# Turning the residual back behind a second batch norm: two more groups of transposes in the waits, products nobody reads between them, and a shorter chain of small operations

## The chip, the core and the metric

The kernel runs on one core of a Trainium2 chip. The metric is the device time of one execution in microseconds (us), the median of several runs. All numbers are float32.

## The reference, cut to what matters

Four graph layers run one after the other on x of shape (128 batches, 64 nodes, 256 features), each as x = x + layer(relu(layernorm(x))). The change sits where the third layer ends and the fourth begins:

```python
# layer 2 (the third)
h = relu(layernorm(x))
agg = A_hat @ h                                   # per batch, 64 x 64
h = relu(batchnorm(agg @ W1.T + b1, g1, be1))     # 512 features
out = batchnorm(h @ W2.T + b2, g2, be2)           # 256 features
x = x + out
# layer 3 (the fourth)
h = relu(layernorm(x))
h = relu(weighting @ (h @ W1)); h = relu(weighting @ (h @ W2)); y = weighting @ (h @ W3)
x = x + y
```

A batch norm takes the mean and variance of a feature over all 8192 tokens. So no token of layer 2 is finished before the last token has gone through its second product: this is a barrier, and layer 3 cannot start before it.

## The kernel before, in words

The 8192 tokens are cut into 16 groups of 512 tokens. x stays in the on-chip memory, tokens on the partitions (tiles `xs[g]`, 4 blocks of 128 tokens by 256 features). Layer 2 works with the features on the partitions: its output tile for group g, `outs[g // 2]`, holds 2 chunks of 128 features by 512 tokens, so that mean and variance are sums along a row.

For each group, the loop of layer 2 applies the first batch norm with its relu on ScalarE (L1039), multiplies on TensorE (L1049, two chunks m), takes the statistics of each product on VectorE (`bn_stats`, L1058) and moves it out of PSUM with its bias on ScalarE (L1059). In the last group the products are sorted so that chunk 0 is complete first. `bn_finish` (L968 on) then makes a scale `sc` and a shift `sh` for each chunk: `bn_aggr`, add eps (L977), power -0.5 on GpSimd (L978), add the bias to the mean (L980), times gamma (L981), mean times scale (L982), beta minus that (L983). The same function finishes the first batch norm (4 chunks) earlier.

Behind the barrier, for each group:

- `normalize(g)` applies scale and shift in place, chunk 0 on ScalarE (L1072), chunk 1 on VectorE (L1075). These two are kept in program order.
- `to_residual(g)` transposes the result back to tokens on the partitions (8 transposes of 128x128 on TensorE, L1085, into two PSUM banks) and adds each bank to `xs[g]` on VectorE (L1089).
- `start(g)` does the layer norm of `xs[g]` (statistics on VectorE at L92 to L98, a power on GpSimd at L96, the scaling with relu on ScalarE at L111, or for one block of group 0 on VectorE at L105 and L109), then the first mix with the weighting (64x64 products, L143) and its two copies out of PSUM (L155, one on VectorE, one on ScalarE). Group 0 is done in two halves of 256 tokens.
- `first_weights`, `second_mix`, `second_weights`, `third_weights`, `last_mix` and `finish` are the rest of layer 3. Each weight product is done as seven smaller products: four first (1, 5, 6, 7), of which 1 and 5 are copied to `p1` and `p5` on ScalarE (L171, L172), then 2, 3 and 4 into the same banks, with sums on VectorE (L174, L175, L183, L187), on GpSimd (L178) and relus on ScalarE (L214, L217).

`bring(n, ahead)` (L1250) puts `to_residual` of n groups and `normalize` of further groups between these stages. Before the first weights of group 0, groups 1 to 3 are normalised, and their 24 transposes stand behind the first four of the seven products; groups 4 and 5 follow behind the second mix, 6 and 7 behind the second weights.

Two resources matter for the order. PSUM has 8 banks, handed out in turn by `bank()`. The pool `ar_right` has 8 tiles, and all of them hold `outs`; the tile `m1` that `first_weights` of group 0 writes `p1` and `p5` into is the tile of groups 0 and 1 of `outs`, free when both have been transposed.

Instructions are issued by each engine in the order that the scheduler wrote down; `issue_after` keeps a stretch behind an instruction.

Of the kernel before, what the change touches and what calls it, by code (L numbers as in the profile page):

```python
# [9 lines left out]
AF = mybir.ActivationFunctionType  # L10
ALU = mybir.AluOpType
# [3 lines left out]
P = 128  # L15
D = 256
# [22 lines left out]
def adj_preln_kernel(ctx: ExitStack, tc: tile.TileContext, x_in, adj, vec, bg0, bg1,  # L39
# [9 lines left out]
    def bank(shape=(P, 512)):  # L49
        return psp.tile(list(shape), F32, tag="ps", name="ps")  # L50
# [50 lines left out]
    def ln_apply(src, dst, rstd, nmr, n=GT, on_vector=()):  # L101

        for t in range(n):
            if t in on_vector:
                nc.vector.tensor_scalar(  # L105
                    dst[:, t, :], src[:, t, :], rstd[:, t : t + 1], nmr[:, t : t + 1],
                    ALU.mult, ALU.add,
                )
                nc.vector.tensor_scalar(dst[:, t, :], dst[:, t, :], 0.0, None, ALU.max)  # L109
                continue  # L110
            nc.scalar.activation(  # L111
                dst[:, t, :], src[:, t, :], AF.Relu,
                bias=nmr[:, t : t + 1], scale=rstd[:, t : t + 1],
            )

    def ln_relu(src, dst, between=None):

# [10 lines left out]
                )  # L128
        return pss

    def mix(src, a2, chunks, dst, copies, swap=False):

        for c0 in range(0, chunks, 2):
            pss = [bank((P, 2, GT, NODES)) for _ in range(2)]
            for t in range(GT):
                for c in range(2):
                    for half in range(2):
                        for b in range(2):  # L140
                            rows = slice(b * 64, b * 64 + 64)
                            col = (c0 + c) * P + half * 64
                            nc.tensor.matmul(  # L143
                                pss[b][half * 64 : half * 64 + 64, c, t, :],
                                lhsT=src[rows, t, col : col + 64],
                                rhs=a2[rows, :],
                                start=True, stop=True,
                            )
            for b in range(2):
                if swap:  # L150
                    to = dst[:, c0 : c0 + 2, :].rearrange("p c (k b m) -> p b c k m", b=2, m=P)
                    last = copies[b](to[:, b], pss[b].rearrange("p c (k q) n -> p c k (q n)", q=2))
                else:
                    to = dst[:, c0 : c0 + 2, :].rearrange("p c (t b n) -> p b c t n", b=2, n=NODES)
                    last = copies[b](to[:, b], pss[b])  # L155
        return last.ins
# [45 lines left out]
    def sums(eng, a11, a12, a21, a22, s1, s2, s3, s4):  # L202

        eng.tensor_tensor(out=s1, in0=a21, in1=a22, op=ALU.add)
        eng.tensor_tensor(out=s2, in0=s1, in1=a11, op=ALU.subtract)
        eng.tensor_tensor(out=s3, in0=a11, in1=a21, op=ALU.subtract)
        eng.tensor_tensor(out=s4, in0=a12, in1=s2, op=ALU.subtract)

    def ends_in(out, func):

# [757 lines left out]
    def bn_finish(st, n, v_0, v_g, v_b, tag):  # L968


        scs, shs = [], []
        for m in range(n):
            mv = bp.tile([P, 2], F32, tag=f"{tag}mv{m}", name=f"{tag}mv{m}")
            sc = bp.tile([P, 1], F32, tag=f"{tag}sc{m}", name=f"{tag}sc{m}")
            sh = bp.tile([P, 1], F32, tag=f"{tag}sh{m}", name=f"{tag}sh{m}")
            nc.vector.bn_aggr(mv, st[:, m].rearrange("p g s -> p (g s)"))
            nc.vector.tensor_scalar(sc, mv[:, 1:2], BN_EPS, None, ALU.add)  # L977
            nc.gpsimd.tensor_tensor(out=sc, in0=sc, in1=mhalf[:, 0:1], op=ALU.pow)  # L978
            mean = mv[:, 0:1]
            nc.vector.tensor_tensor(mean, mean, vecs[:, v_0 + m : v_0 + m + 1], ALU.add)  # L980
            nc.vector.tensor_tensor(sc, sc, vecs[:, v_g + m : v_g + m + 1], ALU.mult)  # L981
            nc.vector.tensor_tensor(sh, mean, sc, ALU.mult)  # L982
            nc.vector.tensor_tensor(sh, vecs[:, v_b + m : v_b + m + 1], sh, ALU.subtract)  # L983
            scs.append(sc)
            shs.append(sh)
        return scs, shs
# [49 lines left out]
    for g in range(NG):  # L1036
        a = h1s[g]
        for m in range(4):
            nc.scalar.activation(  # L1039
                a[:, m, :], a[:, m, :], AF.Relu,  # L1040
                bias=sh1[m], scale=sc1[m],
            )
        pss = [bank() for _ in range(2)]
        order = [(c, m) for c in range(4) for m in range(2)]
        if g == NG - 1:

            order.sort(key=lambda cm: cm[1])
        for c, m in order:
            nc.tensor.matmul(  # L1049
                pss[m], lhsT=w2[c // 2][:, c % 2, m * P : (m + 1) * P], rhs=a[:, c, :],  # L1050
                start=(c == 0), stop=(c == 3),
            )

        if g % 2 == 0:
            outs.append(arena(ar_right))
        o = outs[-1][:, 2 * (g % 2) : 2 * (g % 2) + 2, :]
        for m in range(2):
            nc.vector.bn_stats(st2[:, m, g, :], pss[m])  # L1058
            nc.scalar.activation(  # L1059
                o[:, m, :], pss[m], AF.Identity, bias=vecs[:, V_B2 + m : V_B2 + m + 1]  # L1060
            )
        if g == NG - 4:
            w_three = layer3_weights()
    sc2, sh2 = bn_finish(st2, 2, V_B2, V_G2, V_BE2, "n2")

    b1, t1s, a2, s2s, b3, t3s = w_three

    def normalize(g, tok=slice(0, GN)):

        o = outs[g // 2][:, 2 * (g % 2) : 2 * (g % 2) + 2, tok]  # L1070
        tc.keep_in_program_order(
            nc.scalar.activation(o[:, 0, :], o[:, 0, :], AF.Identity, bias=sh2[0], scale=sc2[0])  # L1072
        )
        tc.keep_in_program_order(
            nc.vector.tensor_scalar(o[:, 1, :], o[:, 1, :], sc2[1], sh2[1], ALU.mult, ALU.add)  # L1075
        )

    def to_residual(g, ks=range(2)):
        o = outs[g // 2][:, 2 * (g % 2) : 2 * (g % 2) + 2, :]
        for k in ks:  # L1080
            ps = bank((P, 2, D))
            for t in range(2):
                tok = (2 * k + t) * P
                for c in range(2):
                    nc.tensor.transpose(  # L1085
                        ps[:, t, c * P : (c + 1) * P], o[:, c, tok : tok + P], ident
                    )
            xk = xs[g][:, 2 * k : 2 * k + 2, :]
            nc.vector.tensor_tensor(xk, xk, ps, ALU.add)  # L1089


    def start(g, behind):


        a = arena(ar_left)
        h = a[:, 0:2, :].rearrange("p a (b d) -> p (a b) d", d=D)
        if g == 0:

            for k in range(2):
                two = slice(2 * k, 2 * k + 2)  # L1100
                with tc.issue_after(scaled) if k else nullcontext():
                    to_residual(0, [k])
                    rstd, nmr, scaled = ln_scale(xs[0][:, two], None, 2, True)
                    ln_apply(xs[0][:, two], h[:, two], rstd, nmr, 2, (1,) if k else ())
        else:
            with tc.issue_after(behind):
                ln_relu(xs[g], h)
        mix(h, w2s, 2, a[:, 2:4, :], (on_vector, on_scalar))
        return a

    def first_weights(a, room):

        h1 = arena(ar_left)
        act = [[a[:, 2 + c, m * HN : (m + 1) * HN] for c in range(2)] for m in range(2)]
        ss = [a[:, i // 2, (i % 2) * HN : (i % 2 + 1) * HN] for i in range(4)]
        sums(nc.vector, *act[0], *act[1], *ss)

        def product(w, b):
            def issue(ps, first):
# [11 lines left out]
            sevens((*act, ss), (*b1, t1s), product), [bank((P, 2, D)) for _ in range(4)], p1, p5,  # L1131
            blocks, ends_in(blocks, AF.Relu), lambda b: [b[:, t] for t in range(2)],
        )()
        return h1

    def second_mix(h1, m1):

# [107 lines left out]

    ready, brought = 1, 1

    def bring(n, ahead):  # L1250


        nonlocal ready, brought
        for _ in range(n):
            if brought < ready:
                to_residual(brought)
                brought += 1
        for _ in range(ahead):
            if ready < NG:
                normalize(ready)  # L1260
                ready += 1

    for k in range(2):
        normalize(0, slice(k * HN, (k + 1) * HN))
    a = start(0, None)
    s3 = None
    for g in range(NG + 1):
        if g == 0:
            bring(0, 3)
        if g < NG:  # L1270

            m1 = arena(ar_right)
            h1 = first_weights(a, m1)
            bring(3 if g == 0 else 1, 2 if g == 0 else 1)
        if s3 is not None:
            pss = [bank((P, 2, D)) for _ in range(2)]
# [1 line left out]
        if g < NG:  # L1278
            second_mix(h1, m1)
            if g == 0:  # L1280
                bring(2, 2)
        if s3 is not None:
            last_mix(pss, s3, 1)
            finish(g - 1, pss)
        if g < NG:
            h2, behind = second_weights(m1, h1)
            bring(2 if g == 0 else 1, 1)
            if g + 1 < NG:
                a = start(g + 1, behind)
            s3 = third_weights(h2)  # L1290
# [52 lines left out]
```

## Time and profile before

| What | Value |
| --- | --- |
| median of 3 runs | 2494.5 us (2494.31 to 2496.09) |
| the profiled execution: time / span | 2495.02 us / 2493.2 us |
| TensorE (PE) matmul busy | 2454.6 us, 98% of the span |
| TensorE weight load (PEld) busy | 2073.4 us, 83% |
| VectorE (DVE) busy | 1516.3 us, 61% |
| ScalarE (ACT) busy | 1145.8 us, 46% |
| GpSimd (POOL) busy | 439.3 us, 18% |
| from 1700 to 1710 us of the span: PE busy, mean clock granted | 4.24 us of 10, 0.63 |
| from 1710 to 1720 us: PE busy, mean clock granted | 9.16 us of 10, 0.69 |

The last two rows are the stretch that the change rewrites: the barrier of the second batch norm lies at 1699 us, the first weights of layer 3 begin at 1710.77 us. "Clock" is the share of full speed that the chip grants TensorE; it is 1.00 in nearly all of the span. A time such as "1701.94" is counted in us from the start of the span. L numbers are lines of the kernel before; in the changed kernel the same lines stand up to 66 further down.

### The profile page before, as it was taken

What the parts mean: (1) busy time and instruction counts of PE and PEld (TensorE: products, weight loads), DVE (VectorE), ACT (ScalarE), POOL (GpSimd) and SP (SyncE); (2) the same over time, 40 slices, a digit from 0 to 9 for tenths busy, and PEclk for the clock granted to TensorE, in tenths of its full rate; (3) what the DMA queues carried; (4) which work ended last, traced back from release to release, by engine and by line L of the source; (5) the groups of instructions that cost most, each with busy time, mean ns of one, the idle gap of its engine ahead of it and who ended that gap; (6) DMA issues with size and microseconds to landing.
All of it is one profiled execution on the core that took longest, in us unless ns stands there. A gap on an engine that the chain in (4) does not pass through costs nothing.

```text
span 2493.2 us, 46254 instructions
## 1 busy us (share of the span) xinstructions
PE 2454.6 (98%) x19614; PEld 2073.4 (83%) x19614; DVE 1516.3 (61%) x2716; ACT 1145.8 (46%) x2027; POOL 439.3 (18%) x368
## 2 busy tenths in 40 slices
PE   8999999999999999999999999998999999999999
PEld 5668888889999998888888864446998898888888
DVE  6658876656566565566599986325556455454544
ACT  4547754444354343444465566743333323333332
POOL 4422211111111111121133331013011111101110
PEclk9999999999999999999999999998999999999999
DMA  3200000001000000000311110010000000000000
GB/s 115 103 2 1 1 17 1 1 1 34 1 1 1 1 1 1 1 13 1 114 39 37 39 32 2 1 59 1 10 9 19 10 10 10 18 10 10 18 9 18
DMA packets 48526, 48.00 MB, mean 19 GB/s; under 512 B 3648, under 2 KB 44736, under 8 KB 48320
## 3 DMA queue, kind: packets, MB, share of 16 engines
q1 hardware_dynamic: 47616, 44.49, 5.8%
q8 instruction: 154, 2.52, 0.4%
q10 hardware_dynamic: 704, 0.56, 0.1%
q14 instruction: 52, 0.43, 0.1%
HBM read 28.26 MB, written 8.39 MB: 15 GB/s over the span
## 4 chain that ended last, share of the span: by engine, by line
PE 87%; DVE 7%; ACT 2%; issue 1%; POOL 1%; DMA 1%; SPq 0%; DVEq 0%; ACTq 0%; POOLq 0%
PE ps L505 40%; PE ps L1157 15%; PE ps L1202 8%; PE ps L1049 4%; PE ps L733 4%; PE ps L143 3%; PE ps L1121 3%; PE ps L451 2%; PE ps L427 2%; PE ps L766 2%; PE ps L788 1%; ACT arena L217 1%; DVE st L92 1%; POOL arena L178 1%; DVE e L831 0%
## 5 line engine op out<-in xcount | busy, mean ns | idle before, releaser
L1157 PE MATMUL ps<-arena 128*128 128x256 f32 x1792 | 393.0, 381 | 1.7 <-DVE arena L198 1.7
L505 PE MATMUL ps<-diff,s 128*128 128x256 f32 (+1 forms) x1824 | 393.5, 371 | 0.9 <-DVE diff L621 0.9
L1157 PEld LDWEIGHTS ps<-arena 128*128 128x128 f32 x1792 | 337.8, 190 | 56.2 <-issue 10.4
L505 PEld LDWEIGHTS ps<-diff,s 128*128 128x128 f32 x1824 | 345.9, 190 | 33.8 <-issue 1.6
L519 ACT ACTIVATE gates<-gates,lbias 128x512 f32<-128x512 f32 (+5 forms) x426 | 244.2, 621 | 202.4 <-DVE gates L183 146.9
L178 POOL TENSOR_TENSOR gates<-p 128x512 f32<-128x512 f32 (+1 forms) x115 | 149.3, 1298 | 882.1 <-DVE p L175 831.0
L505 PE MATMUL ps<-h,w 128*128 128x256 f32 (+1 forms) x1028 | 241.2, 371 | 1.6 <-ACT p L171 1.6
L505 PE MATMUL ps<-diff,w 128*128 128x256 f32 (+1 forms) x1040 | 238.7, 370 | 0.0
L505 PEld LDWEIGHTS ps<-diff,w 128*128 128x128 f32 x1040 | 197.4, 190 | 18.2
L505 PEld LDWEIGHTS ps<-h,w 128*128 128x128 f32 x1028 | 194.6, 190 | 20.9 <-ACT p L171 2.0
L519 ACT ACTIVATE gates<-ps,lbias 128x256 f32<-128x256 f32 (+3 forms) x213 | 91.8, 477 | 247.2 <-PE ps L505 247.1
L217 ACT ACTIVATE arena<-arena 128x512 f32<-128x512 f32 (+1 forms) x160 | 88.6, 582 | 192.6 <-POOL arena L178 103.3
L178 POOL TENSOR_TENSOR arena<-arena 128x512 f32<-128x512 f32 x64 | 72.9, 1139 | 536.2 <-DVE arena L175 536.2
L1202 PE MATMUL ps<-arena 128*128 128x128 f32 x1280 | 149.9, 276 | 0.0
L183 DVE TENSOR_TENSOR gates<-p,ps 128x512 f32<-128x512 f32 (+1 forms) x115 | 76.5, 665 | 120.1 <-PE ps L505 120.1
L1202 PEld LDWEIGHTS ps<-arena 128*128 128x128 f32 x1280 | 145.6, 192 | 1.3 <-issue 0.2
L96 POOL TENSOR_TENSOR rstd<-rstd,mhalf 128x4 f32<-128x4 f32 (+1 forms) x66 | 66.5, 1008 | 411.2 <-DVE rstd L95 402.1
L183 DVE TENSOR_TENSOR arena<-arena,ps 128x512 f32<-128x512 f32 x64 | 39.7, 622 | 149.4 <-PE ps L1157 84.7
L174 DVE TENSOR_TENSOR p<-p,ps 128x512 f32<-128x512 f32 (+1 forms) x131 | 86.8, 663 | 51.2 <-PE ps L505 50.7
L505 PE MATMUL ps<-state,w 128*128 128x256 f32 (+1 forms) x512 | 116.1, 370 | 0.9 <-ACT p L171 0.8
L733 PE MATMUL ps<-arena,w 128*128 128x512 f32 x256 | 114.3, 599 | 1.9 <-ACT arena L155 1.9
L505 PE MATMUL ps<-state,s 128*128 128x256 f32 (+1 forms) x512 | 115.8, 369 | 0.0
(203 smaller groups left out, 4030.9 us busy)
## 6 DMA issues: line engine op xcount, KB each, us to landing
x<-in_x SPq DMA_DIRECT2D x27, 512.0 KB, 6.2
v<-vt SPq DMA_DIRECT2D x128, 64.0 KB, 2.1
out<-x SPq DMA_DIRECT2D x15, 512.0 KB, 2.9
w<-in_wih SPq DMA_DIRECT2D x4, 1024.0 KB, 7.3
w<-in_whh SPq DMA_DIRECT2D x3, 1024.0 KB, 5.5
arena<-in_l3w SPq DMA_DIRECT2D x3, 1024.0 KB, 5.3
w<-in_wqkv SPq DMA_DIRECT2D x1, 768.0 KB, 4.5
x<-in_x SPq DMA_DIRECT2D x2, 256.0 KB, 3.1
```

What stands on the lines that cost most here:

```text
L143: nc.tensor.matmul(pss[b][half * 64 : half * 64 + 64, c, t, :], lhsT=src[rows, t, col : col + 64], rhs=a2[rows, :], start=True, stop=True,)
L174: nc.vector.tensor_tensor(p1, p1, ps[2], ALU.add)
L178: nc.gpsimd.tensor_tensor(out=out[1][1], in0=p1, in1=p5, op=ALU.add)
L183: nc.vector.tensor_tensor(out[0][1], p1, ps[1], ALU.add)
L217: nc.scalar.activation(o, o, func)
L505: nc.tensor.matmul(ps[:, r], lhsT=wc[:, j, :], rhs=bc, start=first and r == 0 and c == 0, stop=True, skip_group_check=True,)
L519: nc.scalar.activation(o, ps, func, bias=lbias[:, col : col + 1])
L733: nc.tensor.matmul(ps, lhsT=w1[:, c, m * P : (m + 1) * P], rhs=a[:, 2 + c, :], start=(c == 0), stop=(c == 1),)
L1049: nc.tensor.matmul(pss[m], lhsT=w2[c // 2][:, c % 2, m * P : (m + 1) * P], rhs=a[:, c, :], start=(c == 0), stop=(c == 3),)
L1121: nc.tensor.matmul(ps[:, t, :], lhsT=w[:, t * P : (t + 1) * P], rhs=b, start=first and t == 0, stop=True, skip_group_check=True,)
L1157: nc.tensor.matmul(ps[:, r, :], lhsT=w[:, c, col : col + P], rhs=b[:, c, :], start=first and r == 0 and c == 0, stop=c == 1, skip_group_ch ...
L1202: nc.tensor.matmul(ps[:, t, :], lhsT=w[:, c, t * P : (t + 1) * P], rhs=b[:, c, :], start=first and t == 0 and c == 0, stop=c == 3, skip_gr ...
```

## The change

It does the following.

1. In `bn_finish` the mean is made negative together with the bias's addition, so that scale and shift need one VectorE operation less per chunk: `sh = -(mean + bias) * sc + beta` is one `scalar_tensor_tensor` in place of two operations. This applies to both batch norms.
2. Group 0's start becomes `first_start`. Groups 0, 1 and 2 are normalised chunk by chunk: chunk 0 of all three on ScalarE as soon as its scale is there (chunk 1's statistics come one stretch of products later), their chunk 0 transposes right behind; then chunk 1 of group 0 on VectorE, of groups 1 and 2 on ScalarE, and their transposes. So six PSUM banks are filled with three groups turned back, and the two other banks are set aside for the first mix.
3. The move of the last product's chunk 1 out of PSUM (`evicted(1)`) is put behind the chunk 0 scalings on ScalarE.
4. `keep_busy` issues products of `ident` with a weight block into a bank whose content has been read; nothing reads them. Four stand behind the last transposes, one behind block 1 and one behind block 3 of the first mix.
5. Group 1's two additions to the residual are put into VectorE's order before and behind the layer norm's last steps; group 2's are put behind the sums of the first weights (`finish_start`).
6. `bring` starts with group 3: groups 3, 4 and 5 behind the first products, 6 and 7 behind the second mix, then one group per stage. Up to group 7, both chunks are normalised on ScalarE; from group 8 on, chunk 1 is on VectorE as it was.

```diff
@@ bn_finish
             mean = mv[:, 0:1]
-            nc.vector.tensor_tensor(mean, mean, vecs[:, v_0 + m : v_0 + m + 1], ALU.add)
+            nc.vector.tensor_scalar(
+                mean, mean, vecs[:, v_0 + m : v_0 + m + 1], -1.0, ALU.add, ALU.mult
+            )
             nc.vector.tensor_tensor(sc, sc, vecs[:, v_g + m : v_g + m + 1], ALU.mult)
-            nc.vector.tensor_tensor(sh, mean, sc, ALU.mult)
-            nc.vector.tensor_tensor(sh, vecs[:, v_b + m : v_b + m + 1], sh, ALU.subtract)
+            nc.vector.scalar_tensor_tensor(
+                sh, mean, sc, vecs[:, v_b + m : v_b + m + 1], ALU.mult, ALU.add
+            )
@@ mix
-            pss = [bank((P, 2, GT, NODES)) for _ in range(2)]
+            pss = banks or [bank((P, 2, GT, NODES)) for _ in range(2)]
             for t in range(GT):
...
+                behind(t, last.ins)
@@ the loop of layer 2
         for m in range(2):
             nc.vector.bn_stats(st2[:, m, g, :], pss[m])
-            nc.scalar.activation(
-                o[:, m, :], pss[m], AF.Identity, bias=vecs[:, V_B2 + m : V_B2 + m + 1]
-            )
+            if (g, m) != (NG - 1, 1):
+                evicted(m)
@@ start of group 0
+    def first_start():
...
+        pss = [[bank((P, 2, D)) for _ in range(2)] for _ in range(3)]
+        mixes = [bank((P, 2, GT, NODES)) for _ in range(2)]
+
+        def keep_busy(n, behind):
+            with tc.issue_after(behind):
+                for _ in range(n):
+                    nc.tensor.matmul(
+                        pss[0][0].rearrange("p t d -> p (t d)")[:, 0:D], lhsT=ident, rhs=b1[0][0],
+                        start=True, stop=True,
+                    )
+
+        for half in halves:
+            normalize(0, half, [0])
+        turn_back(0, pss[0], [0])
+        for g in range(1, 3):
+            normalize(g, chunks=[0])
+            turn_back(g, pss[g], [0])
+        for half in halves:
+            normalize(0, half, [1])
+        for g in range(1, 3):
+            normalize(g, chunks=[1], on_scalar=range(2))
+        evicted(1)
+        lns = []
+        for k in range(2):
+            two = slice(2 * k, 2 * k + 2)
+            with tc.issue_after(lns[0][2]) if k else nullcontext():
+                turn_back(0, pss[0], [1], [k])
+                add_back(0, pss[0], [k])
+                lns.append(ln_scale(xs[0][:, two], None, 2, True))
+        for g in range(1, 3):
+            last = turn_back(g, pss[g], [1])
+        keep_busy(4, last)
+        with tc.issue_after(lns[1][2]):
+            add_back(1, pss[1], [0])
+        for k in range(2):
+            two = slice(2 * k, 2 * k + 2)
+            rstd, nmr, _ = lns[k]
+            applied = ln_apply(xs[0][:, two], h[:, two], rstd, nmr, 2, (1,) if k else ())
+        with tc.issue_after(applied):
+            add_back(1, pss[1], [1])
+        mix(
+            h, w2s, 2, a[:, 2:4, :], (on_vector, on_scalar), banks=mixes,
+            behind=lambda t, last: keep_busy(t % 2, last),
+        )
+        return a, lambda: add_back(2, pss[2])
@@ the order of the stages
-    ready, brought = 1, 1
+    ready, brought = 3, 3
...
-                normalize(ready)
+                normalize(ready, on_scalar=range(2 if ready < NG // 2 else 1))
...
-    for k in range(2):
-        normalize(0, slice(k * HN, (k + 1) * HN))
-    a = start(0, None)
+    a, finish_start = first_start()
...
-            h1 = first_weights(a, m1)
+            h1, summed = first_weights(a, m1)
+            if g == 0:
+                with tc.issue_after(summed):
+                    finish_start()
...
             if g == 0:
-                bring(2, 2)
+                bring(2, 1)
...
-            bring(2 if g == 0 else 1, 1)
+            bring(1, 1)
```

`turn_back` and `add_back` are the two halves of the former `to_residual`: the transposes of given chunks and halves into given banks, and the additions from them.

## The prediction

> **What bounds the kernel now.** I read the page first: TensorE is busy nearly everywhere, and the clock dips in one slice of the 40.
>
> ```profile
> PE 2454.6 (98%) x19614; PEld 2073.4 (83%) x19614; DVE 1516.3 (61%) x2716; ACT 1145.8 (46%) x2027; POOL 439.3 (18%) x368
> PE   8999999999999999999999999998999999999999
> PEclk9999999999999999999999999998999999999999
> ```
>
> So time can only come from the few places where PE waits or runs slowly. The table of windows put the dip at 1700 to 1720 us, and the timeline of PE there shows the stretch that the change rewrites:
>
> ```profile
> 1684.75 14.32 PE L1049 MATMUL ps<-arena,w 128*128 128x512 f32 x33
> 1701.07 0.33 PE L1085 MATMUL ps<-ident,arena 128*128 128x128 f32 x1 [2.00 <-ACT arena L1072]
> 1702.41 1.58 PE L1085 MATMUL ps<-ident,arena 128*128 128x128 f32 x7 [1.02 <-DVE arena L1075]
> 1706.82 1.20 PE L143 MATMUL ps<-w2s,arena 64*64 64x64 f32 x32 [2.83 <-ACT arena L111]
> 1708.79 1.14 PE L143 MATMUL ps<-w2s,arena 64*64 64x64 f32 x32 [0.78 <-ACT arena L111]
> 1710.77 6.44 PE L1121 MATMUL ps<-arena 128*128 128x256 f32 x16 [0.84 <-ACT arena L155]
> 1717.05 1.69 PE L1085 MATMUL ps<-ident,arena 128*128 128x128 f32 x14
> 1718.81 2.86 PE L1121 MATMUL ps<-arena 128*128 128x256 f32 x12
> ```
>
> The reader is to see two things. From 1699.07 (end of L1049) to 1710.77 PE has 4.3 us of work in 11.7 us. And 16 passes of L1121 take 6.3 us until the next work at 1717.05, where 12 of them take 2.7 us: 0.224 each at full clock, near double at half clock. The waits of PE from 1733 us to the end are one line, so behind this stretch every us of PE work removed is a us gained:
>
> ```profile
> PE ps L1157 <- DVE arena L198: 0.4, 2, 0.2
> ```
>
> The windows with the clock say when it is halved. The changes lie at 19.88, 26.70, 1248.68, 1252.08, 1702.64 and 1716.30 us (worked out from the mean clock of the 1 us window around each); all distances are multiples of 3.413 us. So it is decided at fixed edges, by how busy PE was in the window before. Windows between edges (after the length: busy us and count of PE, PEld, DVE, ACT, POOL, then the clock):
>
> ```profile
> 16.48:19.89 3.41, 1.65 (x64) 1.24 (x68) 2.59 (x13) 2.08 (x4) 2.20 (x2) 1.00 1.03 365
> 1289.65:1293.07 3.42, 3.42 (x127) 3.25 (x125) 3.41 (x8) 3.24 (x6) 2.45 (x3) 1.00 0.13 29
> 1473.97:1477.38 3.41, 1.56 (x4) 0.85 (x5) 3.41 (x8) 3.41 (x8) 2.50 (x2) 1.00 0.03 5
> 1699.25:1702.66 3.41, 0.57 (x3) 0.39 (x4) 2.56 (x9) 1.66 (x3) 0.56 (x1) 1.00 0.00 0
> 1709.49:1712.90 3.41, 2.57 (x23) 1.84 (x18) 2.92 (x7) 2.71 (x4) 0.00 (x0) 0.50 0.00 0
> ```
>
> 1.56 us of large products kept the clock (third line), 0.57 lost it (fourth). 2.57, of which 0.45 in 64x64 products, did not bring it back (fifth); 3.42 in the next window did. At 26.70 and 1252.08 full windows brought it back too.
>
> **The change part by part.** The sum is made against the profiled execution, 2495.02 us (span 2493.2 and 1.82 around it), 0.5 above the median 2494.5. I place each instruction at the later of its engine's end and its inputs' end, in the order of instructions of the changed kernel, with durations from the timeline.
>
> *Shorter chains at the batch norms.* One VectorE step between L981 and L983 goes: 0.20 us per chunk (1701.48 to 1701.68). At the second batch norm it counts once, since chunk 1 ends the chain. At the first, the four chunks' chains follow one another on VectorE without a gap (the next `bn_stats`, at 1585.22, 1587.86 and 1590.48, starts where the last ends; its products were complete by 1587.5), so chunk 2 is 0.6 and chunk 3 0.8 earlier. PE waits for just these two:
>
> ```profile
> 1591.46 1.99 PE L1049 MATMUL ps<-arena,w 128*128 128x512 f32 x4 [0.34 <-ACT arena L1039]
> 1594.09 6.28 PE L1049 MATMUL ps<-arena,w 128*128 128x512 f32 x14 [0.64 <-ACT arena L1039]
> ```
>
> With 0.43 per pass PE would be free at 1590.97 and four passes on. The first wait (0.49) goes, since ScalarE is free at 1590.08; the second product starts at 1592.42 + 0.81 + 0.05 = 1593.28, not 1594.09. **Gain 0.81**, kept, as PE bounds the loop behind it.
>
> *Chunk 0 early.* Scale and shift of chunk 0 are ready at 1698.25, before PE's last product ends. ScalarE scales 256 columns in 0.54 and 512 in 0.75, so groups 0, 1, 2 are ready at 1698.9, 1699.4, 1700.1, 1700.9; 12 transposes (0.1135 each at full clock) follow each. The move of chunk 1 (0.69) ends at 1701.6, where ScalarE would wait for the new shift (1701.65): covered. If it came in front, it would cost nothing on the path either, as VectorE scales chunk 1 of group 0. Chunk 1 is ready at 1702.16 (0.20 earlier), and only two transposes stand between it and the addition instead of three and their tails: the addition starts at 1702.61, not 1703.17. **0.56 earlier**, and with it the layer norm: first half of the mix at 1706.25, the second at 1708.23.
>
> *Group 1's two additions* (0.69 each): the first lies in VectorE's wait for GpSimd (0.81 idle before 1707.95); the second runs 1708.39 to 1709.07, behind L109, and the mix's copy on VectorE is behind it. The mix ends at 1708.95, so it costs 0.05 to 0.1. At full clock the second half of the mix takes 0.7 instead of 1.14. First products at **1709.73 instead of 1710.77: gain 1.04**.
>
> *Unread products.* Four are 8 passes, 1.78 us at full clock, 3.55 at half; they start at 1703.7 (or 1704.7) and the mix is queued behind them. At full clock they end at 1705.5: no cost. One more between the mix's halves (0.44) fits into the wait; one behind the mix (0.44) lies beside the copies (0.7).
>
> *The clock at the first products.* If it is full, 16 passes take 3.55 instead of 6.28: **gain 2.73**. The thin window is 1699.2 to 1702.6, now with 12 to 14 transposes, 1.4 to 1.6 us. Do these count? The row: from 1289.65 to 1293.07 PE ran 1.7 us of transposes and 1.7 us of 64x64 products and kept its clock, while 1.65 us of the same small products alone lost it at 19.88:
>
> ```profile
> 1289.56 1.04 PE L250 MATMUL ps<-ident,hc 128*128 128x128 f32 x8
> 1290.43 1.04 PE L126 MATMUL ps<-ident,h 128*128 128x128 f32 x8
> 1291.40 1.16 PE L861 MATMUL ps<-v,eT 64*64 64x64 f32 x64
> 1292.38 0.87 PE L812 MATMUL ps<-k,q 64*64 64x64 f32 x46
> ```
>
> The Trainium skill says the opposite ("TensorE: Matmul & The Clock Gate", section on PE-mode transpose): in transpose mode the full clock does not engage, since it doesn't count as PE-busy the same way. By the rule the clock always falls behind the barrier: the unread products take 3.55 us, the first products start at about 1711.2, and the half clock may last to 1709.5 or 1712.9, so 1.5 to 2.4 of the gain goes. By the row transposes count in part; I take the row. Then, over possible places of the edges, which need not be the same in another run, about two in three leave the first products where I put them (no fall, or a fall that the unread products mend by 1707.5), and one in three costs 1.4 to 1.8.
>
> *The first weights and what follows.* `p1` no longer waits for group 1's transposes (ScalarE idle 5.4 us before 1718.17), but stands behind the mix's copy and six scalings: 1709.41 + 6 x 0.74 = 1713.9. PE has four products to 1713.28 and 9 transposes to 1714.3, then waits 0.15 to 0.25. Products 2 to 4 end at 1717.2, 15 transposes at 1718.9, the second mix (2.1) at 1721.0. ScalarE's next four scalings (to 1721.85) make its copy late by 0.6; on VectorE the copy, four additions, one scaling and two differences then give `t2` at 1727.84. PE, with 16 transposes and 18 passes (4.0), is there at 1726.87 and waits 1.0; before it waited 1.21 for the same, from 1730.6 to 1731.81. The 40 transposes in this stretch are the same number in both. Net of waits: **0 to 0.1**; I take 0. So PE stands 1.04 + 2.73 = 3.8 earlier.
>
> *Two groups fewer behind it.* At this point groups 0 to 7 are turned back, where before it was 0 to 5. 16 transposes leave the dense part: 16 x 0.115 (1.84 for 16 at 1752.17) = **gain 1.84**. The scalings of chunk 1 moved to ScalarE (0.75 each instead of 0.46 on VectorE) fall where I counted them.
>
> Sum: 0.81 + 1.04 + 2.73 + 1.84 = 6.4, so 2495.0 - 6.4 = 2488.6; with 0.2 for joints that are never quite tight, **2488.8 us**.
>
> **The rivals.**
>
> *The clock falls late.* Between the unread products (end 1705.5) and 1709.73 PE has 0.9 us of unread products and 0.6 us of small ones; an edge at 1708.4 to 1709.5 sees some 1.3, near the limit. Half clock for one window from there costs 1.4 to 1.8: 2490.2 to 2490.6. The same time results if it falls at 1702 and is mended only at 1709.
>
> *ScalarE becomes the bound.* It gets ten scalings of 0.74 ahead of the copies that PE waits for. I count 0.2 and an unchanged wait; if `p1` or the mix's copies come 1.5 later, 2490.3. Against it: PE has transposes to do in both places.
>
> *The unread products are a brake (slower than before).* If transposes count for nothing, the clock falls at 1702.6, the 8 passes end at 1708.5, the mix's halves and the two further products follow at half clock to 1711.5, and the first products start at 1712.4, 1.6 later than before. It decides if the clock then comes back only at an edge behind 1719: 16 passes at half clock end at 1719.5, 6.2 behind the forecast, which with transposes at half clock eats the whole gain: 2495.5. Against it: a window full of PE work brought the clock back each time, and the fill makes the windows fuller.
>
> *The change doesn't do what it says:* the fall stays and the early transposes only take up slack: 0.81 + 0.56 + 1.84 leaves 2491.8.
>
> **How the numbers follow.** Forecast 0.60 (own range 2487.8 to 2489.8), late fall 0.20, ScalarE 0.07, clock as before 0.09, brake 0.03, a larger gain, to 2487 (waits at `t2` gone, 1.0), 0.01. The range 2487.3 to 2491.2 leaves out the brake, most of the unchanged clock and the edges of the others. 0.2% is 5.0 us, about what a measurement of this kernel can tell from no change, and the border is 2489.5: nearly all of the forecast case is below it, the other gains are between. Faster 0.64, same 0.34, slower 0.02.
>
> **What would show it.** Right: clock 1.00 from 1709 on; first products near 1709 (all places 0.8 earlier by the first batch norm); 16 passes in about 3.6 us; PE's wait at 1594 about 0.6; `p1` straight behind six scalings; 8 transposes, not 16, in the next bring. Wrong: half clock in the first products, the mix waiting for unread products rather than for L111, or a wait of PE above 1.5 us before `p1` or `t2`.

## The result, and the profile after

Over 14 runs each, the changed kernel takes 2490.91 us (median; 2487.19 to 2492.29) and the kernel before 2495.81 (2494.09 to 2500.74). The ratio is 0.9977 with a 95% interval of 0.9970 to 0.9984: 0.23% faster, 4 to 7.5 us. The forecast time, 2488.8, is 2.1 too low; the range (2487.3 to 2491.2) held the result, 0.3 below its upper end. The three runs of before that were known at first had a median of 2494.5; single runs of one kernel lie 5 to 7 us apart (the last section says what the traces show of that). One run of the kernel before that was measured beside the last two experiments took 10902 us and is left out of their ratios.

The profiled execution took 2489.57 us (span 2487.6). The page again, now without a dip in the clock:

```profile
PE 2450.4 (99%) x19626; PEld 2070.3 (83%) x19626; DVE 1512.0 (61%) x2703; ACT 1149.8 (46%) x2034; POOL 439.3 (18%) x368
PE   7999999999999999999999999999999999999999
PEclk9999999999999999999999999999999999999999
```

The timeline of PE behind the barrier (start, length, engine, line, operation; in brackets how long PE sat idle before and for whom; "passes" are the single instructions that a product is recorded as). L1055 is the former L1049, L1095 the transposes, L1136 the unread products, L144 the mix, L1186 and L1222 the first and second weights:

```profile
1683.63 16.04 PE L1055 MATMUL ps<-arena,w 128*128 128x512 f32 x37
1699.57 0.93 PE L1095 MATMUL ps<-ident,arena 128*128 128x128 f32 x4
1700.76 1.36 PE L1095 MATMUL ps<-ident,arena 128*128 128x128 f32 x8 [0.26 <-ACT arena L1083]
1702.87 1.69 PE L1095 MATMUL ps<-ident,arena 128*128 128x128 f32 x12 [0.75 <-DVE arena L1085]
1704.40 1.89 PE L1136 MATMUL ps<-arena,ident 128*128 128x256 f32 x8
1706.99 0.95 PE L144 MATMUL ps<-w2s,arena 64*64 64x64 f32 x32 [0.70 <-ACT arena L111]
1707.87 0.70 PE L1136 MATMUL ps<-arena,ident 128*128 128x256 f32 x2
1708.96 0.69 PE L144 MATMUL ps<-w2s,arena 64*64 64x64 f32 x32 [0.39 <-ACT arena L111]
1709.59 0.70 PE L1136 MATMUL ps<-arena,ident 128*128 128x256 f32 x2
1710.54 3.69 PE L1186 MATMUL ps<-arena 128*128 128x256 f32 x16 [0.26 <-DVE arena L157]
1714.07 1.15 PE L1095 MATMUL ps<-ident,arena 128*128 128x128 f32 x9
1715.09 2.86 PE L1186 MATMUL ps<-arena 128*128 128x256 f32 x12
...
1723.38 3.62 PE L1222 MATMUL ps<-arena 128*128 128x256 f32 x16
1728.60 6.71 PE L1222 MATMUL ps<-arena 128*128 128x256 f32 x30 [1.60 <-DVE arena L200]
```

What to see: every wait of the old timeline at this place is filled or shorter, the mix waits for L111 and not for the unread products, and the 16 passes of the first products take 3.53 us (1710.54 to 1714.07) instead of 6.28. One wait has grown: 1.60 us for L200 at the second weights. It is the only wait of PE from 1727 us to the end:

```profile
PE ps L1222 <- DVE arena L200: 1.6, 1, 1.6
```

Since executions differ in how late they reach the barrier, I count from the end of PE's last product of layer 2 (1699.07 before, 1699.67 after). All kernels of this study, from one profiled execution each, in us. The six others are told below; 4.36 is 16 passes at full clock with a wait of 0.60 among them:

| Kernel | first weights start | their 16 passes take | end of the span |
| --- | --- | --- | --- |
| before | 11.70 | 6.28 | 794.1 |
| chain_only | 11.38 | 5.61 | 792.4 |
| fill_only | 11.13 | 4.36 | 791.6 |
| no_fill | 11.27 | 5.04 | 789.9 |
| tr_fill | 10.84 | 3.53 | 788.0 |
| changed | 10.87 | 3.53 | 787.9 |
| scal_dve | 10.88 | 4.36 | 788.7 |
| late_adds | 10.89 | 3.53 | 786.2 |

So 6.2 us of the gain lie behind the barrier; 0.55 more lies in front of it, at the first batch norm. These are differences between single executions. The medians give less for the whole, 4.9 us, and the ratio 5.7.

### The profile page after: what moved, and what is told of

The parts are those of the page before. It is cut to its first block, busy times and chain, and to the rows that moved or that the text cites. A ratio compares the mean times of both kernels' runs of the same rounds, so it can differ in the third digit from the quotient of the medians.

```text
span 2487.6 us, 46271 instructions
## 1 busy us (share of the span) xinstructions
PE 2450.4 (99%) x19626; PEld 2070.3 (83%) x19626; DVE 1512.0 (61%) x2703; ACT 1149.8 (46%) x2034; POOL 439.3 (18%) x368
## 4 chain that ended last, share of the span: by engine, by line
PE 87%; DVE 7%; ACT 2%; POOL 2%; issue 1%; DMA 0%; SPq 0%; DVEq 0%; POOLq 0%; ACTq 0%
PE ps L507 40%; PE ps L1222 16%; PE ps L1267 8%; PE ps L1055 4%; PE ps L735 4%; PE ps L144 3%; PE ps L1186 3%; PE ps L429 2%; PE ps L453 2%; PE ps L768 2%; PE ps L790 1%; ACT arena L219 1%; DVE st L92 1%; POOL rstd L96 1%; POOL arena L180 1%
## 5 line engine op out<-in xcount | busy, mean ns | idle before, releaser
L1222 PE MATMUL ps<-arena 128*128 128x256 f32 x1792 | 392.6, 381 | 1.6 <-DVE arena L200 1.6
L1222 PEld LDWEIGHTS ps<-arena 128*128 128x128 f32 x1792 | 338.0, 190 | 55.7 <-issue 11.2
L1267 PE MATMUL ps<-arena 128*128 128x128 f32 x1280 | 149.7, 276 | 0.0
L1267 PEld LDWEIGHTS ps<-arena 128*128 128x128 f32 x1280 | 145.5, 192 | 1.1
```

Source lines behind the costliest of these rows:

```text
L1222: nc.tensor.matmul(ps[:, r, :], lhsT=w[:, c, col : col + P], rhs=b[:, c, :], start=first and r == 0 and c == 0, stop=c == 1, skip_group_ch ...
L1267: nc.tensor.matmul(ps[:, t, :], lhsT=w[:, c, t * P : (t + 1) * P], rhs=b[:, c, :], start=first and t == 0 and c == 0, stop=c == 3, skip_gr ...
```

## The experiments

The theory (A) was the forecast's: shorter chains, a clock kept full by transposes and unread products together, and two groups of transposes taken out of the dense part. The rivals are named in the expectations.

**The shorter chain alone (chain_only)**: the kernel before with the edits of `bn_finish`.

```diff
-            nc.vector.tensor_tensor(mean, mean, vecs[:, v_0 + m : v_0 + m + 1], ALU.add)
+            nc.vector.tensor_scalar(
+                mean, mean, vecs[:, v_0 + m : v_0 + m + 1], -1.0, ALU.add, ALU.mult
+            )
-            nc.vector.tensor_tensor(sh, mean, sc, ALU.mult)
-            nc.vector.tensor_tensor(sh, vecs[:, v_b + m : v_b + m + 1], sh, ALU.subtract)
+            nc.vector.scalar_tensor_tensor(
+                sh, mean, sc, vecs[:, v_b + m : v_b + m + 1], ALU.mult, ALU.add
+            )
```

> Kernel before with the shorter chain in the batch norms alone. Theory A (the forecast's sum): the first batch norm's last product starts 0.8 us earlier, PE's two waits there go from 0.49 + 0.91 to 0 + 0.5 or 0.6, the second batch norm gives 0.2 more; about 1.0 us in all, clock at the first weights as before (16 passes in about 6.3 us where a window's edge lies as it did). Rival B (the chains are hidden, the whole gain is the clock and the transposes): nothing, PE's waits at the first batch norm as before.

Measured: ratio 0.9995 (0.9987 to 1.0004), medians 2494.9 and 2495.86, which can't tell 1 us from none. The trace can. PE at the first batch norm:

```profile
1591.21 5.51 PE L1052 MATMUL ps<-arena,w 128*128 128x512 f32 x12
1597.23 3.27 PE L1052 MATMUL ps<-arena,w 128*128 128x512 f32 x7 [0.51 <-ACT arena L1042]
```

The first of the two waits is gone and the second is left: 6.02 us from the first product to the fourth chunk's, where before it was 6.56 (1587.53 to 1594.09), a gain of 0.54. A is right in kind but forecast half as much again (0.81); B is wrong. The durations say why. The operation that went had freed 0.20 us, but the two that stayed do more (`mean` at L980, `sh` at L984):

```profile
1590.19 0.20 DVE L980 TENSOR_SCALAR n1mv<-n1mv,vecs 128x1 f32<-128x1 f32 x1
...
1591.13 0.22 DVE L984 SCALAR_TENSOR_TENSOR n1sh<-n1mv,n1sc,vecs 128x1 f32<-128x1 f32 x1
```

They take 0.20 and 0.22 instead of 0.15 and 0.16. The longer L980 costs nothing, as VectorE waits for GpSimd behind it anyway (0.55 idle instead of 0.60); the longer L984 ends the chain and takes 0.06 of the 0.20 back. 0.14 is left per chunk: the next `bn_stats` follows after 2.50 and 2.48 us instead of 2.64 and 2.62. Behind the barrier this kernel also ends 1.7 us earlier than before; 0.7 of this is a window's edge that fell better (5.61 for the 16 passes), another 0.76 is a surprise told in the last section.

**The unread products alone (fill_only)**: the kernel before with `keep_busy` in group 0's start (cut to the calls; `kept` holds the banks and the last transposes of group 0's halves).

```diff
+        if g == 0:
...
+            keep_busy(4, kept[1][1])
+            mix(h, w2s, 2, a[:, 2:4, :], (on_vector, on_scalar),
+                behind=lambda t, last: keep_busy(t % 2, last))
+            return a
         mix(h, w2s, 2, a[:, 2:4, :], (on_vector, on_scalar))
```

> Kernel before with the unread products alone (four behind group 0's transposes, one behind the second and one behind the fourth block of the first mix), no group turned back early, old chain. Theory A: the clock still falls behind the barrier (the thin window has only 0.6 us of work), but the unread products bring it back one or two windows later, so that the 16 passes of the first products take 3.6 to 4.5 us instead of 6.3; the eight passes at half clock (3.5 us) may hold the mix back by up to 1 us. Net 1.5 to 2.7 us faster. Rival C (brake): the mix waits for them and the clock is still half at the first products, which start 1 us later: no gain, or up to 2 us slower.

Measured: ratio 0.9997 (0.9989 to 1.0005), medians 2494.87 and 2495.86. That interval holds no gain as well as one of 2.7 us. In the trace this kernel takes 2.5 us less behind the barrier.

```profile
1707.23 3.39 PE L1113 MATMUL ps<-arena,ident 128*128 128x256 f32 x8 [0.27 <-DVE x L1090]
1710.55 0.69 PE L143 MATMUL ps<-w2s,arena 64*64 64x64 f32 x32
...
1713.69 1.10 PE L1135 MATMUL ps<-arena 128*128 128x256 f32 x4 [0.26 <-DVE arena L156]
1715.39 2.83 PE L1135 MATMUL ps<-arena 128*128 128x256 f32 x12 [0.60 <-DVE arena L205]
```

The clock falls at 1706.7, the eight passes run at half clock (3.39 us) and bring it back at 1710.1; the mix waits for them (no bracket in the second line), but only 0.2 us later than before. The brake (C) exists in this profile and costs that much. At full clock PE overtakes VectorE, which does three scalings (1.45 us) before the sums: 0.60 of wait. So the fill alone gives the clock back, and part of it goes into the next wait.

**Without the unread products (no_fill)** and **with transposes in their place (tr_fill)**: the changed kernel with one loop edited. The edit of tr_fill is shown; no_fill keeps the product and has `range(0)`.

```diff
-                for _ in range(n):
-                    nc.tensor.matmul(
-                        pss[0][0].rearrange("p t d -> p (t d)")[:, 0:D], lhsT=ident, rhs=b1[0][0],
-                        start=True, stop=True,
-                    )
+                for _ in range(4 * n):
+                    nc.tensor.transpose(pss[0][0][:, 0, 0:P], ident, ident)
```

> Changed kernel without its unread products. Theory A: the early transposes alone don't carry the clock over the 6 us from the last transposes to the first products, in which only 1 us of small products is left; a window of 3.4 us lies in it wherever the edges are, the clock is half at the start of the first products, their 16 passes take 4.5 to 6.4 us instead of 3.5, and the kernel loses 1 to 2.8 us of the changed kernel's gain. Rival D (the early transposes keep the clock by themselves, the unread products are idle): 16 passes in 3.5 us, time as the changed kernel.

> Changed kernel with each unread product replaced by four unread transposes of the identity (as long on PE: 16 x 0.1135 = 1.8 us for the first four). Theory A (transposes count as work for the clock): 16 passes of the first products in 3.5 to 4 us and the time of the changed kernel. Rival E (the rule that transposes do not count as busy): clock and time as without unread products, 16 passes in 4.5 to 6.4 us, 1 to 2.8 us slower than the changed kernel.

Measured: no_fill 2492.87 against 2495.86, ratio 0.9988 (0.9981 to 0.9995); tr_fill 2489.44, ratio 0.9977 (0.9969 to 0.9985). The stretch from the last transposes to the first products, and these products, first of no_fill, then of tr_fill (in the windows, the first number is the length, then busy us and count of PE, PEld, DVE, ACT, POOL, then the clock):

```profile
1705.83:1712.21 6.38, 2.33 (x64) 1.91 (x65) 5.19 (x17) 2.44 (x5) 1.40 (x2) 0.70 0.01 3
1712.21:1717.25 5.04, 5.04 (x17) 4.16 (x18) 2.72 (x6) 5.02 (x8) 0.00 (x0) 0.70 0.00 0
```

```profile
1703.96:1710.07 6.11, 4.70 (x90) 3.74 (x89) 5.35 (x18) 2.44 (x5) 1.40 (x2) 1.00 0.01 3
1710.07:1713.60 3.53, 3.53 (x16) 3.07 (x17) 2.72 (x6) 3.53 (x6) 0.00 (x0) 1.00 0.00 0
```

Without the fill the clock was half from 1708.4 to 1715.3, the products took 5.04 us, and 1.9 us of the gain behind the barrier were gone: theory A, not D. With transposes as fill the clock stayed full, and the stages are as with products, to 0.1 us: theory A, not E. The medians, measured side by side, say the same: 2492.87 without fill, 2489.44 with transposes.

The edges of the windows show it without any fill as well. In no_fill the clock fell at 1708.44, so with the spacing of 3.413 us that the prediction worked out, the two windows before it are these:

```profile
1701.61:1705.03 3.42, 2.35 (x17) 1.60 (x16) 2.46 (x9) 3.07 (x5) 0.55 (x1) 1.00 0.00 0
1705.03:1708.44 3.41, 0.98 (x17) 0.67 (x19) 3.08 (x13) 0.92 (x3) 0.70 (x1) 1.00 0.00 0
```

In the first PE ran transposes and nothing else (all 17 are L1095), and the clock stayed at 1.00 behind it; in the second it ran 0.98 us, and the clock fell. In fill_only a window with 1.11 us of transposes alone (1703.28 to 1706.69) lost it. So transposes count for the clock here, and the prediction was right to take the row and not the rule.

**VectorE's additions later (late_adds)**, to name the wait that grew: groups 6 and 7 are turned back where they were, and their additions issued behind the differences of the second weights.

```diff
-    def second_weights(m1, room):
+    def second_weights(m1, room, between=lambda: None):
...
         last = differences(nc.vector, *act[0], *act[1], *ts)
+        with tc.issue_after(last):
+            between()
...
             if g == 0:
-                bring(2, 1)
+                for _ in range(2):
+                    late.append((brought, [bank((P, 2, D)) for _ in range(2)]))
+                    turn_back(*late[-1])
+                    brought += 1
+                bring(0, 1)
...
-            h2, behind = second_weights(m1, h1)
+            h2, behind = second_weights(m1, h1, lambda: [add_back(*x) for x in late])
```

> Changed kernel with the four additions of groups 6 and 7 behind VectorE's differences of the second weights instead of in front of them (same instructions, same transposes). Theory F (PE's wait of 1.60 us for the second difference is VectorE working off 2.5 us of additions that nobody needs yet): the wait goes to 0 to 0.2 us, the other stages as in the changed kernel, 1.4 to 1.6 us faster than it. Rival G (the additions then stand in front of the sums that free PE's banks): PE waits as long a little later, no gain.

Measured: 2489.0 against 2497.2, ratio 0.9966 (0.9952 to 0.9979), in the trace 1.8 us less than the changed kernel behind the barrier. VectorE in the changed kernel, then in this one:

```profile
1723.73 0.68 DVE L154 COPY arena<-ps 128x512 f32<-128x512 f32 x1
1724.33 2.47 DVE L1103 TENSOR_TENSOR x<-x,ps 128x512 f32<-128x512 f32 x4
1726.72 0.54 DVE L1085 TENSOR_SCALAR arena<-arena,n2sc,n2sh 128x512 f32<-128x512 f32 x1
1727.17 0.68 DVE L199 TENSOR_TENSOR arena<-arena 128x512 f32<-128x512 f32 x1
1727.78 0.68 DVE L200 TENSOR_TENSOR arena<-arena 128x512 f32<-128x512 f32 x1
```

```profile
1727.69 0.69 DVE L200 TENSOR_TENSOR arena<-arena 128x512 f32<-128x512 f32 x1
1728.41 0.69 DVE L202 TENSOR_TENSOR arena<-arena 128x512 f32<-128x512 f32 x1
1729.02 2.47 DVE L1103 TENSOR_TENSOR x<-x,ps 128x512 f32<-128x512 f32 x4
```

L200 comes at 25.8 us behind the barrier instead of 28.1, and PE has no wait left from 1727 us on; no other took its place. Theory F, not G. Behind the barrier this version is the shortest of the study, though the intervals of the two ratios overlap: the trace, one execution of each, is what sets them apart.

**Chunk 1 back on VectorE (scal_dve)**:

```diff
-                normalize(ready, on_scalar=range(2 if ready < NG // 2 else 1))
+                normalize(ready)
```

> Changed kernel with chunk 1 of groups 3 to 7 scaled on VectorE, as in the kernel before, instead of on ScalarE (first_start unchanged). Theory H (the scalings are only balanced between two engines that both have room): p1's copy stands behind three scalings instead of six, but the sums of the first weights stand behind three VectorE scalings, so that PE, at full clock, waits about 0.6 us for them as in the kernel with the unread products alone; the copies of the second mix come 1.4 us earlier on ScalarE, and VectorE does two more scalings in its place: wait at the second difference 1.2 to 1.6. In all 0.3 to 1 us slower than the changed kernel. Rival I (the ten scalings on ScalarE are what makes PE wait at the second difference): that wait falls to under 0.5 us and the kernel is 0.5 to 1 us faster than the changed one.

Measured: 2492.2 against 2497.2, ratio 0.9980 (0.9972 to 0.9987); 0.8 us more than the changed kernel behind the barrier.

```profile
1713.98 5.42 PE L1186 MATMUL ps<-arena 128*128 128x256 f32 x24 [0.60 <-DVE arena L206]
...
1730.89 4.34 PE L1222 MATMUL ps<-arena 128*128 128x256 f32 x19 [1.39 <-DVE arena L200]
```

A wait of 0.60 for the sums, as in fill_only, and 1.39 instead of 1.60 for L200; another 0.24 is a wait for ScalarE at 1968.77 that the changed kernel does not have. Theory H: putting chunk 1 on ScalarE removes the wait that the full clock would otherwise meet, and is not what makes PE wait later.

## Why the prediction was right, and where a step was off

- *Which way and how much.* Forecast against the profiled execution: 6.4 us, or 0.2 less. The stages that the change touches sum to 0.55 + 6.2 = 6.75 in the traces. That this is so close is in part luck: 0.76 of it is a gain that I didn't foresee (the pauses of the last section), and without it the terms give 6.0, each within 0.3 of its forecast. The two spans differ by 5.6, since this execution came 1.15 us later to the first batch norm, up to which both kernels are the same.
- *The chains.* 0.81 forecast for the first batch norm, 0.55 measured. The term was mis-sized: I took out an operation at its price (0.20) and let the remaining ones keep theirs, and the last of them grew by 0.06.
- *The start of the first weights.* 1.04 earlier forecast, 0.83 measured. The addition came 0.42 earlier, not 0.56: again the chain, 0.14 instead of 0.20, and the last transposes. The mix at full clock and VectorE's addition in front of its copy were as counted.
- *The clock.* 2.73 forecast, 2.75 measured. It was the right call for the right reason: no_fill shows that the early transposes don't suffice, tr_fill that transposes count. The windows behind the barrier held 2.35 us of transposes in no_fill and 2.36 in the changed kernel (1700.40 to 1703.82), not the 1.4 to 1.6 that I counted with the old edges. The rival that the clock falls late did not show in the profiles of the changed kernel, tr_fill, late_adds or scal_dve. In these four an edge of the windows lay 0.7 to 0.8 or 1.6 to 1.7 us behind the last product of layer 2 (counted in steps of 3.413 us from a change of the clock elsewhere in the same execution). Other positions no profile with both the early transposes and a fill has shown, so the one chance in three of a late fall is not refuted; late falls in a part of the executions would fit a median gain below that of the traces, but that is not shown. Fill_only shows the fall in the first thin window, mended by the fill.
- *The wait at the second weights.* Forecast 1.0, measured 1.60. L200 ends 28.8 us behind the barrier, as worked out; but PE was there earlier, since I carried over 18 passes in front of that wait, and the new order has 16. The two passes (0.44) come behind it. The prediction named a wait above 1.5 us before `t2` as a sign of being wrong, and this is one. The net of this stretch was put at nothing, and it is small: from the end of the 16 passes to the products behind the wait PE takes 14.53 us instead of 14.76, but with the two passes it would be 14.97. The rival that ScalarE becomes the bound is not what made the wait: scal_dve takes five of the ten scalings from ScalarE and still waits 1.39, late_adds moves four additions on VectorE and has no wait. The wait of 0.15 to 0.25 forecast before products 2 to 4 did not come.
- *Two groups fewer behind it.* 1.84 forecast, 2.4 measured from the end of that wait to the end of the span, although those two passes are now in this part. PE has 7188 instructions there instead of 7202, which is 16 transposes fewer and two passes more. 0.76 of the gain has nothing to do with groups: chain_only has it too (the pauses of the last section). What is left for the transposes is 2.39 - 0.76 + 0.44, about 2.1; no run takes the two groups out alone.
- *The unread products cost nothing*: at 1706.3 they were done, 0.7 before the mix could start.
- *The time itself.* I anchored at 2495.02, one execution, and the median of three, 2494.5. With 14 runs before lies at 2495.81, so 0.8 of the miss of 2.1 is the anchor. The other 1.3 is that the medians show a gain of 4.9 where 6.2 was forecast; the ratio, 0.9977, would make it 5.7. That the result lies inside the range, 0.3 from its end, is in part luck too, with runs of one kernel 5 us apart.

## What to carry to other kernels

When an engine's clock depends on how busy it is, a barrier costs twice: the wait itself, and the slow start behind it. Work that is due anyway is the best fill, unread work does the rest, as long as it ends before the real work is ready. And once the bound engine is faster, look at what stands in front of its next input on the other engines: four additions that nobody was waiting for cost 1.6 us here, and moving them gave that back in the trace.

## What the runs showed of the hardware

- *Transposes keep the clock.* 24 unread transposes of 128x128 (16 in 1.91 us, then twice 4) held it at 1.00 as 12 passes of products did, and a window with 2.35 us of transposes alone kept it. The Trainium skill ("TensorE: Matmul & The Clock Gate", section on PE-mode transpose) says they don't count the same way; here the measurement decides. One thing stays open: the profile records these transposes as MATMUL, and they take as long as products of the same shape (16 in 1.91 us; 48 products of L1267 in 5.62), so it does not show whether they run in the mode that the page means.
- *A pause without a wait.* In the kernel before and in fill_only, VectorE stands idle for 0.46 or 0.47 us in one place each of two groups, the same two places in both kernels, with nothing to wait for in the profile; in other groups it is some 0.1 us there. PE then waits for it:

```profile
2163.56 0.69 DVE L196 TENSOR_TENSOR arena<-arena 128x512 f32<-128x512 f32 x1 [0.46 <-DVE arena L152]
...
2260.55 0.69 DVE L197 TENSOR_TENSOR arena<-arena 128x512 f32<-128x512 f32 x1 [0.47 <-DVE arena L152]
...
2263.19 20.96 PE L1157 MATMUL ps<-arena 128*128 128x256 f32 x96 [0.23 <-DVE arena L198]
```

  Both groups take PE 47.96 us instead of 47.61. In all six kernels with the shorter chain, which have 6 to 13 VectorE instructions fewer, both pauses are gone from PE's path. What causes them is open; no run tested it.
- *The spread lies mostly elsewhere.* The eight profiled executions reached the barrier between 1699.1 and 1702.6 us, and they had drifted apart by 3.7 us before the first line that differs between the kernels. The clock explains a part: about 1477 us it was halved for one window in four of the eight, and these four lost 1.5 to 1.7 us there. In some it was halved at 17 to 29 and about 1250 us too. The clock does not explain all: the execution of the changed kernel has no halved window on record before the barrier, that of the kernel before has three ahead of the first batch norm, and yet the changed kernel came there 1.15 us later. In it PE stood idle for 1.38 us before 1427.30, with nothing to wait for in the profile, where the kernel before did not; what it was is open. So a gain of a few us is read from stages, and the whole only from many runs.
